# A four-layer preact network on one core: where layer 3 keeps its chain results, and which engine does its small work

## The chip, the cores and the metric

The kernel runs on one core of one Trainium2 chip. The metric is the device time of one execution in microseconds (us), the median of several runs. Five engines work at once, each in the order of its own queue: TensorE (matmuls), VectorE, ScalarE, GpSimd, and SyncE (SP), which here only issues DMA transfers. Matmul results go to PSUM, eight banks of 512 float32 columns per partition; everything else lies in SBUF.

## What is computed

The input x has shape (4, 256, 48, 48), float32. Four layers each add a branch to x, every branch starting with a group norm over 32 groups: layer 0 is cosine attention with 8 heads, layer 1 a gate from pooled depthwise convolutions, layer 2 non-local attention whose output is batch-normalised. Layer 3 is the one that changes:

```python
def _L3_conv_ref(x, attn_w1, attn_w2, refine_w, refine_b):   # x is the group norm's result
    p = jnp.mean(x, axis=(2, 3))
    h = leaky_relu(p @ attn_w1.T, 0.01)
    a = sigmoid(h @ attn_w2.T)                               # a gate for each image and channel
    y = x * a[:, :, None, None]
    y = depthwise_conv3x3(y, refine_w, padding="SAME") + refine_b[None, :, None, None]
    mu = jnp.mean(y, axis=(2, 3), keepdims=True)
    var = jnp.mean(jnp.square(y - mu), axis=(2, 3), keepdims=True)
    y = (y - mu) * rsqrt(var + 1e-5)
    return leaky_relu(y, 0.01)
...
x = x + _L3_conv_ref(_gn(x), ...)
```

## The kernel before, in words

The order of layer 3 is written out by hand: every engine executes its instructions in the order in which the Python code emits them, and semaphores between engines follow the data. An access to a PSUM bank is ordered against every access of another engine to the same bank, whatever the columns.

**Tiles.** Four images times two halves of 128 channels make eight tiles, i = 0 to 7. Two tiles of one image are a pair. A tile is 48 x 48 pixels in six slices of 384 pixels; two slices are a group g, which fills one of three convolution PSUM tiles (`cv_tile`, two banks each). Each bank has 512 columns, of which a slice uses 384.

**A tile's way.** `w_product` (L1504) makes on TensorE what layer 2 adds to a third of a tile, in the PSUM tile `w_all` (rows of the profile call it `w`), of which there is one. `grow` (L1558, VectorE) adds it to x and writes the padded image `pads`; `border` (GpSimd) writes the rim; ScalarE's `square` (L1582) sums squares for the group norm. The padded image is then spread into three shifted copies, `shifted` (`sh`): `spread_out` by eight transfers for each half image from SP (L1596), `keep_here` by copies on VectorE (L1602) or ScalarE (L1598). `products` (L1719) convolves a slice from these copies: 24 small matmuls. ScalarE's `evict` (L1731) and `square` (L1742) take a group out and sum it and its squares; `moments`, `scales`, `shift` (VectorE, with a `pow` on GpSimd at L179) make the scale and offset; `scale` (L1796, ScalarE) applies them; `leak` (L1802) and `gain` (L1807), both VectorE, apply the leaky ReLU and add the block's input; `store` (SP, L1813) writes the group out. The last tile is treated apart: VectorE's `stats` (L1762) reads its moments from PSUM, and nothing is evicted before scaling.

**The chain.** For each pair a `Chain` makes the group norm's scale and the gate in nine short steps: VectorE `total`, TensorE `groups` (L1645), VectorE `inverse`, VectorE `pooled`, TensorE `first_layer` (L1660), VectorE `hidden`, TensorE `second_layer` (L1674), ScalarE `gate`, VectorE `scaled`. The three TensorE results, and that of a check on the attention sums (`judge`, `sound`, L1832 and L1835), lie in `g_tile()`, the last 128 columns of the second bank of `w_all`.

**The schedule.** Time is counted in steps: step t is slice t of the 48 (`CONV`), so tile i begins at step 6 i. `at(t, rank, fn)` puts a piece of work at a step, and within a step the pieces are emitted by rank: FRONT, CONV, PRODUCT, GROW, MID, EVICT, SMALL, MOMENTS, SQUARE, SCALE, LAST, PLACE, STORE. `GATE_AT` gives the steps of the chain against the first step of its pair, `HERE` the steps and engines of the copies, `put_tile` the rest. A tile is prepared by `put_before` 12 steps ahead, a product in each of three steps.

**Before the loop.** Tiles 0 and 1 are prepared in straight code: tile 0's three products into the three convolution tiles, tile 1's first into `w_all` and the others into convolution tiles that have come free. `hum` (L195) issues filler matmuls. The zeros in `shifted` (32 partitions x 2600) are written by GpSimd's memset (L1511, L1856).

**After the loop.** The last tile's statistics and scales come first, then leaks, sums and stores of what is left over from tile 6 (`late`), then those of tile 7.

Of the kernel before, what the change touches and what calls it, by code (L numbers as in the profile page):

```python
# [9 lines left out]
F32 = mybir.dt.float32  # L10
AF = mybir.ActivationFunctionType
# [67 lines left out]
def usual_path(  # L79
# [112 lines left out]
    def hum(out, n):  # L192

        for _ in range(n):
            nc.tensor.matmul(out, lhsT=gmat, rhs=gmat, start=True, stop=True)  # L195
# [1267 lines left out]
    def w_tile():  # L1463
        return [w_all[:, 0, :SL], w_all[:, 1, :SL]]

    def g_tile():
        return w_all[:, 1, SL:]

    def cv_tile():
        return ps_cv.tile([P, 2, 512], F32, tag="cv", name="cv")  # L1470

    def w_pair():
        both = cv_tile()
        return [both[:, 0, :SL], both[:, 1, :SL]]
# [33 lines left out]
        return ps  # L1508


    nc.gpsimd.memset(shifted[0][0:32, 2:4, :], 0.0)  # L1511
    first = [cv_tile() for _ in range(L2C)]
    of_groups = first[L2C - 1][:, 0, SL : SL + B * NK]
    first = [w_product(0, c, [ps[:, 0, :SL], ps[:, 1, :SL]]) for c, ps in enumerate(first)]
    ahead = [w_tile()]
    hum(ahead[0][0][:, :P], 11)

    nc.vector.tensor_mul(sc2, sc2, vec[:, V_G2, :])
    nc.vector.tensor_mul(bi2, bi2, sc2)
# [13 lines left out]
        of_groups, lhsT=gmat, rhs=means.rearrange("p b k -> p (b k)"), start=True, stop=True  # L1533
    )
    w_product(1, 0, ahead[0])
    hum(g_tile(), 5)
    gm = lp.tile([P, B, NK], F32, name="gm")
    edge = lp.tile([P, B, NK], F32, name="edge")
    minus = lp.tile([P, B, NK], F32, name="minus")
    dev = lp.tile([P, B, NK], F32, name="dev")  # L1540
    dev2 = lp.tile([P, B, NK], F32, name="dev2")

    def edges():
        nc.vector.tensor_copy(gm.rearrange("p b k -> p (b k)"), of_groups)
# [7 lines left out]
    def grow(i, c, ps, halves=range(2)):  # L1552

        n, k = TILES[i]
        xs = XT[SEQ[n]][:, k, :].rearrange("p (h r c) -> p h r c", h=2, c=HW)
        to = inside(i, c)
        for h in halves:
            nc.vector.scalar_tensor_tensor(  # L1558
                to[:, h], ps[h].rearrange("p (r c) -> p r c", c=HW),
                sc2[:, k : k + 1], xs[:, h, c * RS : (c + 1) * RS, :], ALU.mult, ALU.add,  # L1560
            )
# [65 lines left out]
    class Chain:  # L1627
# [5 lines left out]
        def steps(self):  # L1633
# [49 lines left out]
            def scaled():  # L1683
# [6 lines left out]
                nc.vector.tensor_mul(self.rsa2, self.rsa, self.rsa)  # L1690

            steps = [
                (MID, total), (SMALL, groups), (FRONT, inverse), (MID, pooled),
                (SMALL, first_layer), (FRONT, hidden), (SMALL, second_layer), (FRONT, gate),
                (FRONT, scaled),
            ]
# [2 lines left out]
    class Conv:  # L1699
# [9 lines left out]
        def products(self, s):  # L1709
            g, h = s // 2, s // L2C  # L1710
            if s % 2 == 0:
                self.ps[g] = cv_tile()
            out = self.ps[g][:, s % 2, :SL].rearrange("p (r c) -> p r c", c=HW)
            sh = shifted[(2 * self.i + h) % 3].rearrange("p j (r c) -> p j r c", c=W2)
            r0 = (s % L2C) * RS
            for dr in range(3):
                for j in range(4):
                    held = slice(0, HELD[j])
                    nc.tensor.matmul(  # L1719
                        out[32 * j : 32 * j + 32], lhsT=made["taps3"][held, self.k, dr, j, :],  # L1720
                        rhs=sh[held, j, r0 + dr : r0 + dr + RS, 0:HW],
                        start=dr == 0, stop=dr == 2,
                    )
# [22 lines left out]

        def moments(self):

            self.mv = mv = small.tile([P, 2], F32, tag="in_mv", name="in_mv")
            nc.vector.tensor_reduce(mv, self.st, AX.X, ALU.add)  # L1750
            nc.vector.tensor_scalar(mv, mv, 1.0 / N, None, ALU.mult)
            d = small.tile([P, 1], F32, tag="in_d", name="in_d")
            nc.vector.tensor_add(d, mv[:, 0:1], self.c)
            ve = small.tile([P, 1], F32, tag="in_ve", name="in_ve")
            nc.vector.scalar_tensor_tensor(ve, d, -1.0, d, ALU.mult, ALU.mult)
            nc.vector.tensor_add(mv[:, 1:2], mv[:, 1:2], ve)

        def stats(self, s):

# [5 lines left out]
            self.mv = small.tile([P, 2], F32, tag="in_mv", name="in_mv")  # L1765
            nc.vector.bn_aggr(self.mv, self.bn.rearrange("p s f -> p (s f)"))

        def scales(self):
            k, ch = self.k, self.chain
            ve = small.tile([P, 1], F32, tag="in_ve2", name="in_ve2")  # L1770
            nc.vector.tensor_scalar(
                ve, self.mv[:, 1:2], ch.rsa2[:, k : k + 1], IN_EPS, ALU.mult, ALU.add
            )
# [4 lines left out]
            rb = vec[:, V_RB, k : k + 1]  # L1778
            nc.vector.scalar_tensor_tensor(
                my, self.mv[:, 0:1], ch.rsa[:, k : k + 1], rb, ALU.mult, ALU.add  # L1780
            )
            self.off = small.tile([P, 1], F32, tag="in_off", name="in_off")
            nc.vector.tensor_sub(self.off, rb, my)

        def shift(self):
            k = self.k
            self.sc = small.tile([P, 1], F32, tag="in_sc", name="in_sc")
            nc.vector.tensor_mul(self.sc, self.chain.rsa[:, k : k + 1], self.ri)
            self.sf = small.tile([P, 1], F32, tag="in_sf", name="in_sf")
            nc.vector.tensor_mul(self.sf, self.off, self.ri)  # L1790

        def scale(self, g, fr=None):
            z = self.cols(g)
# [10 lines left out]
        def gain(self, g):  # L1804
            z = self.cols(g).rearrange("p (r c) -> p r c", c=HW)
            r0 = 1 + 2 * RS * g
            nc.vector.scalar_tensor_tensor(  # L1807
                z, rows_of(self.i)[:, r0 : r0 + 2 * RS, 1 : 1 + HW],
                bi2[:, self.k : self.k + 1], z, ALU.add, ALU.add,
            )  # L1810

        def store(self, g, eng=None):
# [6 lines left out]
    def judge():  # L1819
# [17 lines left out]
        return [(0, MID, lows), (2, SMALL, count), (3, FRONT, compare)]  # L1837

    GATE_AT = {
        0: (3, 4, 5, 5, 8, 9, 10, 11, 12), B - 1: (-2, -1, 0, 0, 2, 3, 4, 5, 6),  # L1840
    }
    for n in range(1, B - 1):
        GATE_AT[n] = (-1, 2, 4, 4, 8, 9, 10, 11, 12)
    chains = [Chain(n) for n in range(B)]
    convs = [Conv(i) for i in range(len(TILES))]

# [5 lines left out]
    grow(0, L2C - 1, first[L2C - 1], [0])  # L1852
    grow(0, 0, first[0], [1])
    spread_first(0)
    for sh in shifted[1:]:
        nc.gpsimd.memset(sh[0:32, 2:4, :], 0.0)  # L1856
    for c in range(1, L2C):
        grow(0, c, first[c], [1])
    spread_first(1)
    centres()  # L1860
    noted[0]()
    for c in range(L2C):
        square(0, c)
    for c in range(L2C):
        grow(1, c, ahead[c])
        if c + 1 < L2C:
            ahead.append(w_product(1, c + 1, w_pair()))
            hum(g_tile(), 3)
        square(1, c)
    border(1)  # L1870


# [11 lines left out]
    def put_before(t, i):  # L1884
# [9 lines left out]
            at(t - 11 + c, SQUARE, lambda c=c: square(i, c))  # L1894
        at(t - 12, PLACE, lambda: border(i))

    late = []
    HERE = [
        (-6, 0, (0, 1), "dve"), (-5, 0, (2, 3), "dve"),
        (-3, 1, (0, 1), "act"), (-3, 1, (2,), "dve"), (-2, 1, (3,), "dve"),  # L1900
    ]

    def put_tile(t, cv, final):
        for s in range(NSL):
            at(t + s, CONV, lambda s=s: cv.products(s))
        if final:
            for s in range(NSL - 1):
                at(t + s + 1, MOMENTS, lambda s=s: cv.stats(s))
            return
        for g in range(NG3):  # L1910
            at(t + 2 * g + 2, EVICT, lambda g=g: cv.evict(g))
            at(t + 2 * g + 3, SQUARE, lambda g=g: cv.square(g))
        at(t + 2, EVICT, cv.centre)
        soon = t + 2 * NSL == T
        t += 0 if soon else 2 if cv.k else 5
# [16 lines left out]
    T = len(convs) * NSL  # L1932
    for i, cv in enumerate(convs):
        t = i * NSL
        put_tile(t, cv, i == len(convs) - 1)
# [875 lines left out]
```

## Time and profile before

| what | us |
|---|---|
| median of 3 runs | 3540.59 (3536.17 to 3544.25) |
| the profiled execution | 3540.24 |
| its span, first to last instruction | 3538.5 |
| layer 3 up to its first convolution slice | 3357.1 to 3380.9 |
| 48 slices | 3380.9 to 3518.3 |
| from the last slice to the end | 3518.3 to 3538.5 |

The profile is one execution. Its page lists busy time by engine, the idle time of an engine ahead of a group of instructions with what released it, and DMA queues; the trace behind it can be asked for a timeline, for waits, for a chain of releases that ended last, and for busy times in given stretches (the windows view). A row such as `PE L1660 MATMUL w<-pm,w 128*64 128x1 f32 x4` is engine, line, operation, output and inputs by the program's names, shape, and count. Names are shared: `x` stands for the images and results, `w` for `w_all` and for weights.

### The profile page before, as it was taken

How to read it: one execution, taken by the hardware profiler on the slowest of the kernel's cores; microseconds unless marked ns; L12 is line 12 of the kernel's file. 1: busy time of each engine (PE TensorE's matmuls, PEld its weight loads, DVE VectorE, ACT ScalarE, POOL GpSimd, SP SyncE). 2: the span in 40 equal slices, each digit the busy share in tenths (PEclk: the TensorE clock that was granted, in tenths of full speed). 3: DMA queues.
4: the chain of work that ended last, by engine and by line, in shares of the span. 5: the costliest groups of instructions: out<-in, count | busy, mean ns of one | idle time of the engine just before them, and what ended most of it. 6: DMA issues, size and time to landing. Idle time of an engine off the chain costs nothing. (4 is left out here: it accounts for less than half of the span.)

```text
span 3538.5 us, 88557 instructions
## 1 busy us (share of the span) xinstructions
PE 3439.1 (97%) x37144; PEld 1743.7 (49%) x37144; DVE 2567.9 (73%) x3523; ACT 2369.3 (67%) x3843; POOL 774.9 (22%) x591
## 2 busy tenths in 40 slices
PE   9999999999999999999999999999999999899986
PEld 5554555454444444444444444444444445565532
DVE  3555545467788788787887886878878868656877
ACT  5665666665886796558867975579668755555465
POOL 2333333321111010010110110110100116666520
PEclk9999999999999999999999999999999999999998
DMA  2211111111111111221111111111111100000066
GB/s 89 49 26 22 26 22 26 22 26 22 27 26 22 26 22 26 56 45 22 26 21 26 21 26 21 26 22 26 22 22 22 22 8 5 5 8 7 4 169 205
DMA packets 121753, 116.62 MB, mean 33 GB/s; under 512 B 58833, under 2 KB 112705, under 8 KB 120577
## 3 DMA queue, kind: packets, MB, share of 16 engines
q1 hardware_dynamic: 120240, 109.16, 16.3%
q8 instruction: 293, 4.80, 0.6%
q10 hardware_dynamic: 1104, 1.71, 0.1%
q14 instruction: 116, 0.94, 0.1%
HBM read 56.99 MB, written 11.80 MB: 19 GB/s over the span
## 5 line engine op out<-in xcount | busy, mean ns | idle before, releaser
L315 ACT ACTIVATE pt<-sc 128x768 f32<-128x768 f32 x1944 | 1475.0, 811 | 731.7 <-PE sc L309 724.1
L355 DVE TENSOR_TENSOR acc<-acc,pt 128x768 f32<-128x768 f32 x1368 | 1370.2, 1002 | 173.7 <-ACT pt L315 74.7
L329 PE MATMUL av<-pt,v 64*64 64x384 f32 x13824 | 1275.7, 484 | 0.0
L309 PE MATMUL sc<-q,k 64*64 64x384 f32 x13824 | 1269.8, 482 | 0.5 <-ACT pt L315 0.5
L309 PEld LDWEIGHTS sc<-q,k 64*64 64x64 f32 x13824 | 524.8, 133 | 590.5 <-issue 544.7
L329 PEld LDWEIGHTS av<-pt,v 64*64 64x64 f32 x13824 | 517.7, 133 | 600.8 <-issue 567.4
L410 POOL TENSOR_TENSOR o<-o,rinv 128x384 f32<-128x384 f32 x95 | 115.6, 1217 | 1729.6 <-DMA rinv<-rinv 1725.2
L340 POOL TENSOR_TENSOR half<-pt 128x768 f32<-128x768 f32 x189 | 365.1, 1935 | 535.8 <-ACT pt L315 496.5
L700 DVE SCALAR_TENSOR_TENSOR x<-pj,bo,x 128x384 f32<-128x384 f32 x192 | 118.5, 617 | 314.4 <-PE pj L687 312.9
L355 DVE TENSOR_TENSOR acc<-acc,half 128x768 f32<-128x768 f32 x171 | 184.1, 1076 | 216.6 <-POOL half L340 216.0
L876 ACT ACTIVATE prod<-pd,wt 128x256 f32<-128x256 f32 x486 | 337.2, 765 | 0.2
L604 PE MATMUL pj<-xs,w 128*128 128x384 f32 (+1 forms) x720 | 275.4, 505 | 0.0
L604 PEld LDWEIGHTS pj<-xs,w 128*128 128x128 f32 x720 | 124.1, 189 | 127.9 <-issue 38.9
L329 PE MATMUL av<-pt,qv 64*64 64x384 f32 x1728 | 176.5, 498 | 0.0
L309 PE MATMUL sc<-qv,kd 64*64 64x384 f32 x1728 | 171.1, 486 | 2.4 <-ACT pt L315 2.4
L899 DVE TENSOR_REDUCE prod<-prod 128x256 f32<-128x1280 f32 x114 | 168.7, 1480 | 0.7 <-ACT prod L876 0.7
L687 PE MATMUL pj<-o,wo 128*128 128x384 f32 (+1 forms) x384 | 160.6, 502 | 5.8 <-issue 3.6
L635 PEld LDWEIGHTS pj<-w,xs 128*128 128x128 f32 x1080 | 134.5, 191 | 24.1 <-issue 1.2
L349 DVE TENSOR_TENSOR acc<-pt 128x768 f32<-128x768 f32 x99 | 112.8, 1140 | 39.8 <-ACT pt L315 39.8
L406 POOL TENSOR_TENSOR o<-raw 128x384 f32<-128x384 f32 x95 | 126.9, 1336 | 52.0 <-ACT raw L402 51.6
L635 PE MATMUL pj<-w,xs 128*128 128x128 f32 x1080 | 134.9, 275 | 0.0
L402 ACT COPY raw<-av 128x768 f32<-128x768 f32 x108 | 86.4, 800 | 48.3 <-PE av L329 44.9
(265 smaller groups left out, 2398.4 us busy)
## 6 DMA issues: line engine op xcount, KB each, us to landing
xs<-in_x_dram SPq DMA_DIRECT2D x90, 384.0 KB
sh<-pad SPq DMA_DIRECT2D x126, 162.2 KB
rinv<-rinv SPq DMA_DIRECT2D x208, 94.5 KB
out_dram<-x SPq DMA_DIRECT2D x24, 384.0 KB
l<-row SPq DMA_DIRECT2D x416, 1.5 KB
w<-in_wqkv_dram SPq DMA_DIRECT2D x32, 192.0 KB
x<-in_x_dram SPq DMA_DIRECT2D x4, 1152.0 KB
x<-in_x_dram SPq DMA_DIRECT2D x9, 384.0 KB
```

The source lines that it names most:

```text
L309: nc.tensor.matmul(ps[c * D : (c + 1) * D, h, :SL], lhsT=u["of"]["k"][r, j0 : j0 + D], rhs=u["of"]["q"][r, u["qc"]], start=True, stop=True,)
L315: nc.scalar.activation(pt, ps[:, :, :SL], AF.Exp, scale=u["scale"])
L329: nc.tensor.matmul(u["av"][h * D : (h + 1) * D, half, :SL], lhsT=value(u, j, h)[r], rhs=pt[r, h, :], start=j == 0, stop=j == JB - 1,)
L340: nc.gpsimd.tensor_add(half, pts[0], pts[1])
L355: nc.vector.tensor_add(u["acc"], u["acc"], term)
L406: eng.tensor_add(u["sum"], u["raw"][:, 0, :], u["raw"][:, 1, :])
L604: nc.tensor.matmul(ps[:, :n], lhsT=at["w"][:, k, t, :], rhs=xs[s][:, k, :n], start=k == 0, stop=k == NK - 1,)
L635: nc.tensor.matmul(ps[:, i * P : (i + 1) * P], lhsT=xs[s][:, k, i * P : (i + 1) * P], rhs=at["w"][:, k, 2, :], start=k == 0, stop=k == NK - 1,
L687: nc.tensor.matmul(ps[:, :n], lhsT=wo[:, p, k * P : (k + 1) * P], rhs=o["o"][:, :n], start=True, stop=True,)
L700: nc.vector.scalar_tensor_tensor(xs, ps[:, :SL], pair["bo"][:, k : k + 1], xs, ALU.add, ALU.add)
L876: nc.scalar.activation(bufs[n % 3][:, :, min(n, 1) + i].rearrange("p (r c) -> p r c", c=AS), pd[:, PAD + dr : PAD + dr + AS, PAD + dc : PA ...
L899: nc.vector.tensor_reduce(to, bufs[n % 3][:, :, : min(n, 1) + len(taps)], AX.X, ALU.add)
```

## The change

All edits are in layer 3.

- `g_tile()` returns the last 128 columns of the second bank of the convolution tile in use instead of those of `w_all`, and the chain's and the check's steps move (`GATE_AT`, `put_chain(13, ...)`), so that their matmuls come after an odd slice. `inverse` has rank MID.
- `moments`, `scales` and `shift` are issued to GpSimd, with each fused operation in two, other than those of the last tile. Steps of scales, leaks and sums move by one to two.
- One of the four copies of a second half image moves from VectorE to ScalarE.
- ScalarE clears the three `shifted` buffers, ahead of everything else, instead of GpSimd.
- Filler falls from 11 to 3 ahead of the means, and the others move; tile 1's products all precede the loop's other work, `centres` comes earlier, and the sums of the last attention rows (`noted`) later.
- Tile 6's leaks, sums and stores all go behind the last slice. Of the six sums there, three (tile 6's groups 1 and 2, tile 7's group 0) leave VectorE: TensorE adds the leaked values and the block's input in PSUM by an identity matrix (`keep_up`, `join`), and ScalarE adds `bi2` and takes them out; the other three stay with `gain`. One store goes out from ScalarE's queue.

```diff
+    cv_last = {}
     def g_tile():
-        return w_all[:, 1, SL:]
+        return cv_last["ps"][:, 1, SL:]
...
-    nc.gpsimd.memset(shifted[0][0:32, 2:4, :], 0.0)
+    for sh in shifted:
+        nc.scalar.activation(
+            sh[0:32, 2:4, :].rearrange("p j c -> p (j c)"),
+            gmat[0:32, 0:1].to_broadcast([32, 2 * CH]), AF.Identity, scale=0.0,
+        )
...
-    hum(ahead[0][0][:, :P], 11)
+    hum(ahead[0][0][:, :P], 3)
...
     w_product(1, 0, ahead[0])
-    hum(g_tile(), 5)
...
+    for c in range(1, L2C):
+        ahead.append(w_pair())
+        hum(ahead[c][0][:, :P], 5 if c == 1 else 1)
+        w_product(1, c, ahead[c])
...
-                (MID, total), (SMALL, groups), (FRONT, inverse), (MID, pooled),
+                (MID, total), (SMALL, groups), (MID, inverse), (MID, pooled),
...
-                self.ps[g] = cv_tile()
+                self.ps[g] = cv_last["ps"] = cv_tile()
...
+            eng, st = nc.gpsimd, self.st
-            nc.vector.tensor_reduce(mv, self.st, AX.X, ALU.add)
-            nc.vector.tensor_scalar(mv, mv, 1.0 / N, None, ALU.mult)
+            eng.tensor_add(mv, st[:, :, 0], st[:, :, 1])
+            eng.tensor_add(mv, mv, st[:, :, 2])
+            eng.tensor_scalar(mv, mv, 1.0 / N, None, ALU.mult)
-            nc.vector.tensor_add(d, mv[:, 0:1], self.c)
-            nc.vector.scalar_tensor_tensor(ve, d, -1.0, d, ALU.mult, ALU.mult)
-            nc.vector.tensor_add(mv[:, 1:2], mv[:, 1:2], ve)
+            eng.tensor_add(d, mv[:, 0:1], self.c)
+            eng.tensor_mul(d2, d, d)
+            eng.tensor_sub(mv[:, 1:2], mv[:, 1:2], d2)
...
-        def scales(self):
+        def scales(self, eng=None):
+            eng = eng or nc.gpsimd
...
+        def onto(self, g, ps, ins, first):
+            for h in range(2):
+                nc.tensor.matmul(
+                    ps[:, h, :SL].rearrange("p (r c) -> p r c", c=HW), lhsT=ident,
+                    rhs=ins[:, h * RS : (h + 1) * RS, :], start=first, stop=not first,
+                )
+        def keep_up(self, g, ps):
+            r0 = 1 + 2 * RS * g
+            self.onto(g, ps, rows_of(self.i)[:, r0 : r0 + 2 * RS, 1 : 1 + HW], True)
+        def join(self, g, ps):
+            self.onto(g, ps, self.cols(g).rearrange("p (r c) -> p r c", c=HW), False)
+            nc.scalar.activation(
+                self.cols(g).rearrange("p (h s) -> p h s", h=2), ps[:, :, :SL], AF.Identity,
+                bias=bi2[:, self.k : self.k + 1],
+            )
...
-        0: (3, 4, 5, 5, 8, 9, 10, 11, 12), B - 1: (-2, -1, 0, 0, 2, 3, 4, 5, 6),
+        0: (3, 5, 6, 7, 9, 10, 11, 12, 13), B - 1: (-2, -1, 0, 0, 3, 4, 5, 6, 7),
-        GATE_AT[n] = (-1, 2, 4, 4, 8, 9, 10, 11, 12)
+        GATE_AT[n] = (-2, 1, 2, 3, 5, 6, 9, 10, 11)
...
-    for sh in shifted[1:]:
-        nc.gpsimd.memset(sh[0:32, 2:4, :], 0.0)
     for c in range(1, L2C):
         grow(0, c, first[c], [1])
+    centres()
     spread_first(1)
-    centres()
-    noted[0]()
...
         grow(1, c, ahead[c])
-        if c + 1 < L2C:
-            ahead.append(w_product(1, c + 1, w_pair()))
-            hum(g_tile(), 3)
         square(1, c)
+    noted[0]()
...
-        (-3, 1, (0, 1), "act"), (-3, 1, (2,), "dve"), (-2, 1, (3,), "dve"),
+        (-3, 1, (0, 1), "act"), (-2, 1, (2,), "act"), (-2, 1, (3,), "dve"),
...
-        t += 0 if soon else 2 if cv.k else 5
+        t += 0 if soon else 1 if i == len(convs) - 3 else 3 if cv.k else 5 if t == 0 else 4
         at(t + 8, FRONT, cv.moments)
-        at(t + 8, FRONT, cv.scales)
+        at(t + 8, MOMENTS, cv.scales)
...
-            if soon and g == NG3 - 1:
-                late.append((cv, g))
+            if soon:
                 continue
-            u = t + 10 + g + (not soon and cv.k)
+            u = t + (10 if t == 5 else 11) + g
...
-    put_chain(14, judge())
+    put_chain(13, judge())
...
-    cv.scales()
-    cv.shift()
+    cv.scales(nc.vector)
+    was = convs[-2]
+    was.leak(0)
+    cv.shift(nc.vector)
     for g in range(NG3):
         cv.scale(g, cv.ps[g])
-    for t in sorted(events):
-        for _, fn in sorted(events[t], key=lambda job: job[0]):
-            fn()
-    for tile, g in late + [(cv, g) for g in range(NG3)]:
-        tile.leak(g)
-        tile.gain(g)
-        tile.store(g)
+    was.keep_up(1, w_all)
+    was.leak(1)
+    was.join(1, w_all)
+    was.leak(2)
+    was.gain(0)
+    was.store(0)
+    was.store(1)
+    cv.leak(0)
+    was.keep_up(2, w_all)
+    cv.keep_up(0, cv.ps[0])
+    was.join(2, w_all)
+    cv.join(0, cv.ps[0])
+    cv.leak(1)
+    cv.gain(1)
+    cv.store(1)
+    was.store(2)
+    cv.leak(2)
+    cv.gain(2)
+    cv.store(2)
+    cv.store(0, nc.scalar)
```

More of the change, by code (lines that the diff above doesn't have):

```diff
@@ L1747, in moments @@
         def moments(self):
+            eng, st = nc.gpsimd, self.st
             self.mv = mv = small.tile([P, 2], F32, tag="in_mv", name="in_mv")
-            nc.vector.tensor_reduce(mv, self.st, AX.X, ALU.add)
-            nc.vector.tensor_scalar(mv, mv, 1.0 / N, None, ALU.mult)
+            eng.tensor_add(mv, st[:, :, 0], st[:, :, 1])
+            eng.tensor_add(mv, mv, st[:, :, 2])
+            eng.tensor_scalar(mv, mv, 1.0 / N, None, ALU.mult)
             d = small.tile([P, 1], F32, tag="in_d", name="in_d")
-            nc.vector.tensor_add(d, mv[:, 0:1], self.c)
-            ve = small.tile([P, 1], F32, tag="in_ve", name="in_ve")
-            nc.vector.scalar_tensor_tensor(ve, d, -1.0, d, ALU.mult, ALU.mult)
-            nc.vector.tensor_add(mv[:, 1:2], mv[:, 1:2], ve)
+            eng.tensor_add(d, mv[:, 0:1], self.c)
+            d2 = small.tile([P, 1], F32, tag="in_d2", name="in_d2")
+            eng.tensor_mul(d2, d, d)
+            eng.tensor_sub(mv[:, 1:2], mv[:, 1:2], d2)
         def stats(self, s):
@@ L1766, in aggregate @@
             nc.vector.bn_aggr(self.mv, self.bn.rearrange("p s f -> p (s f)"))
-        def scales(self):
+        def scales(self, eng=None):
             k, ch = self.k, self.chain
+            eng = eng or nc.gpsimd
             ve = small.tile([P, 1], F32, tag="in_ve2", name="in_ve2")
-            nc.vector.tensor_scalar(
-                ve, self.mv[:, 1:2], ch.rsa2[:, k : k + 1], IN_EPS, ALU.mult, ALU.add
-            )
+            rb = vec[:, V_RB, k : k + 1]
+            if eng is nc.gpsimd:
+                eng.tensor_mul(ve, self.mv[:, 1:2], ch.rsa2[:, k : k + 1])
+                eng.tensor_scalar(ve, ve, IN_EPS, None, ALU.add)
+            else:
+                eng.tensor_scalar(
+                    ve, self.mv[:, 1:2], ch.rsa2[:, k : k + 1], IN_EPS, ALU.mult, ALU.add
+                )
             self.ri = small.tile([P, 1], F32, tag="in_ri", name="in_ri")
@@ L1777, in scales, with shift @@
             my = small.tile([P, 1], F32, tag="in_my", name="in_my")
[L1778 to L1781, printed above, removed]
+            if eng is nc.gpsimd:
+                eng.tensor_mul(my, self.mv[:, 0:1], ch.rsa[:, k : k + 1])
+                eng.tensor_add(my, my, rb)
+            else:
+                eng.scalar_tensor_tensor(
+                    my, self.mv[:, 0:1], ch.rsa[:, k : k + 1], rb, ALU.mult, ALU.add
+                )
             self.off = small.tile([P, 1], F32, tag="in_off", name="in_off")
-            nc.vector.tensor_sub(self.off, rb, my)
-        def shift(self):
+            eng.tensor_sub(self.off, rb, my)
+        def shift(self, eng=None):
             k = self.k
+            eng = eng or nc.gpsimd
             self.sc = small.tile([P, 1], F32, tag="in_sc", name="in_sc")
-            nc.vector.tensor_mul(self.sc, self.chain.rsa[:, k : k + 1], self.ri)
+            eng.tensor_mul(self.sc, self.chain.rsa[:, k : k + 1], self.ri)
             self.sf = small.tile([P, 1], F32, tag="in_sf", name="in_sf")
-            nc.vector.tensor_mul(self.sf, self.off, self.ri)
+            eng.tensor_mul(self.sf, self.off, self.ri)
         def scale(self, g, fr=None):
@@ L1809, in gain @@
                 bi2[:, self.k : self.k + 1], z, ALU.add, ALU.add,
+            )
+        def onto(self, g, ps, ins, first):
[3 more added lines that the diff above has]
+                    rhs=ins[:, h * RS : (h + 1) * RS, :], start=first, stop=not first,
+                )
+        def keep_up(self, g, ps):
[6 more added lines that the diff above has]
+                bias=bi2[:, self.k : self.k + 1],
             )
@@ L1895, in put_before, with put_tile @@
         at(t - 12, PLACE, lambda: border(i))
-    late = []
     HERE = [
         (-6, 0, (0, 1), "dve"), (-5, 0, (2, 3), "dve"),
-        (-3, 1, (0, 1), "act"), (-3, 1, (2,), "dve"), (-2, 1, (3,), "dve"),
+        (-3, 1, (0, 1), "act"), (-2, 1, (2,), "act"), (-2, 1, (3,), "dve"),
     ]
-    def put_tile(t, cv, final):
+    def put_tile(i, t, cv, final):
         for s in range(NSL):
@@ L1934, in usual_path @@
         t = i * NSL
-        put_tile(t, cv, i == len(convs) - 1)
+        put_tile(i, t, cv, i == len(convs) - 1)
         if i > 1:
```

## The prediction

> **What bounds the kernel now.** I read the page first: TensorE is busy 97% of 3538.5 us, but the diff only touches what follows the last attention block, from about 3357 us. So I cut that stretch in the windows view, at the head, the four pairs of tiles (12 steps each, one convolution slice a step) and the tail. Columns: TensorE, weight loads, VectorE, ScalarE, GpSimd busy us (instructions), TensorE clock, DMA share, GB/s.
>
> ```profile
> 3357.10:3380.90 23.80, 14.04 (x112) 8.87 (x112) 18.15 (x44) 9.19 (x14) 16.02 (x14) 0.82 0.42 99
> 3380.90:3413.60 32.70, 31.43 (x351) 12.25 (x354) 18.48 (x36) 21.88 (x41) 1.70 (x5) 0.97 0.67 164
> 3413.60:3454.50 40.90, 33.88 (x356) 12.73 (x352) 32.78 (x70) 28.18 (x49) 4.06 (x7) 0.92 0.75 206
> 3454.50:3493.70 39.20, 32.60 (x352) 14.81 (x344) 32.17 (x66) 28.30 (x50) 2.96 (x5) 0.96 0.85 240
> 3493.70:3518.30 24.60, 24.57 (x297) 9.81 (x296) 22.15 (x58) 16.79 (x28) 2.33 (x4) 1.00 0.64 183
> 3518.30:3538.50 20.20, 0.00 (x0) 0.00 (x0) 14.88 (x23) 4.40 (x5) 0.54 (x1) 0.60 0.38 149
> ```
>
> The same twelve steps take 32.7, 40.9 and 39.2 us; the last pair, which prepares no tile, takes 24.6. TensorE should set the pace and does not. Its timeline says why (the bracket is idle time and releaser):
>
> ```profile
> 3376.24 1.65 PE L195 MATMUL w<-gmat 128*128 128x128 f32 x6 [8.17 <-DVE pad L1558]
> ...
> 3424.84 0.38 PE L1645 MATMUL w<-gn_sq,gmat 128*128 128x2 f32 x2 [2.12 <-DVE pad L1558]
> 3425.16 4.20 PE L1719 MATMUL cv<-sh,taps 96*32 96x384 f32 x48
> ...
> 3444.58 0.59 PE L1660 MATMUL w<-pm,w 128*64 128x1 f32 x4 [3.77 <-DVE pad L1558]
> 3445.10 6.90 PE L1719 MATMUL cv<-sh,taps 96*32 96x384 f32 x48
> ```
>
> Filler (L195) and chain matmuls (L1645, L1660) write a corner of the bank w, and wait until VectorE's `grow` (L1558) has read *other* columns of it. After the 3.77 us wait 48 convolution matmuls take 6.90 instead of 4.08: the wait is paid again in a halved clock.
>
> **What the Trainium skill says.** "PSUM — Partial Sum Buffer", PSUM bank collisions: engines must be kept apart by bank, not by address. The trace agrees: the chain waits for reads of disjoint columns. "TensorE: Matmul & The Clock Gate", What's actually happening: an idle window of some 3.4 us halves the clock. Agrees: 0.50 after 3.77 us, no slowing after 2.12. "SBUF — State Buffer", Who interferes with whom: GpSimd shares a port pair with VectorE's fast copies and two-input operations, and the later one blocks. Agrees: two VectorE copies at 3368.7 us took 1.93 and 2.88 us beside GpSimd instead of 0.83, and GpSimd's border copy 0.92 to 1.00 instead of 0.32. "ScalarE: Activation LUTs", What ACT_TABLE_LOAD costs: an ACTIVATE costs 186 ns + 0.833 ns per element; the 1298-element copy at 1.27 us agrees.
>
> **Head.** ScalarE clears three buffers. By that price 2600 elements are 2.35 us each; three are 7.1 us from 3356.9 (where GpSimd's memset starts now, released by the same VectorE work) to 3364.0. ScalarE is then idle until its copies at 3366.76, so this is free; if it takes 8.5 us it still just fits. Filler of 11 becomes 3 (22 to 6 instructions at 0.12 us: -1.9), which lets the group matmul come when the means are ready; VectorE's 1.09 us wait before L1544 goes. Today the pads are ready for the spread at 3366.7; then 3365.6. All of tile 1's products now precede the loop and no filler waits for L1558: that takes away the 8.17 us wait and the filler and product behind it. What is late next is the spread of the first half: six of its transfers go out from 3365.7; at the 250 GB/s that the DMA moved at 3369 to 3375, 6 x 162 KB is 3.9 us, with about 1 us before the first byte and 1 us after: 3371.6. ScalarE's three copies (3.87 us) end at 3369.5, GpSimd's two (3.24) at 3368.9, TensorE's own queue at 3368.7. Convolution starts at 3371.6 instead of 3380.9: **-9.3 us** (bounds -5 and -10: ScalarE's clears late by 4 us, or an earlier DMA).
>
> **Loop.** Now 3380.9 to 3518.3, 137.4 us. Removed waits of TensorE: first layer 1.27 + 2 x 3.77, groups 2 x 2.12, judge 0.21 + 0.30: 13.6. Removed slow clock: 6.90 - 4.08 = 2.8, and 1.6 after the other 3.77 us wait: 4.4. The initial slow slice (2.96 for 2.14) costs 0.8, which I count as gone since the idle time before it falls from 8 to 3 us. Small product waits (1.3) I leave in. Sum -18.8: 118.6 us, near the bare work: 48 slices x 2.03 + 18 products x 0.81 + chains 4.9 = 116.9. The chain's new places are all after an odd slice, when the convolution bank is complete and its successor is another bank, so its readers hold up nothing but the later eviction.
>
> What then becomes tight, per pair against TensorE's 30.4 us (12 x 2.03 + 6 x 0.81 + 1.2):
> - VectorE: busy 32.5 now. It loses seven or eight small operations per tile, 1.6 to 1.9 us, and one 0.83 us copy: 2 x 2.6 = 5.2, leaving 27.4, plus waits for `pow` of about 1 us.
> - GpSimd gets some 15 tiny operations per tile. No row has such arithmetic; the nearest are border copies at 0.27 to 0.32 and `pow` at 0.55, so 4 to 5 us per tile, up to 15 if every one waits behind a VectorE operation of 1 us. It idles over 85% of the loop. A gain lengthened from 1.02 to 1.11 us beside a border copy gives 0.09 us per GpSimd operation on VectorE: 2 x 17 x 0.09 = 3 per pair (bounds 0 and 0.4 each). VectorE: 31.
> - ScalarE: 28.2 plus two copies of 1.27: 30.8. Evictions have four steps (over 8 us) of room and scales two steps, so its queue may slip 3 to 4 us unseen.
> - DMA: 0.75 x 40.9 + 0.85 x 39.2 = 64 us of service for two pairs, against 61 us. Spreads have six steps, some 14 us, from issue to need, so most is hidden. SP still waits for a store before each reload; queued behind that are eight spreads, with 5 us of room.
>
> All four are near 30 us and coupled through in-order queues. I take 32, 33, 33 and 25 us for the pairs: 123 us, **-14.4** (bounds 117.5 and 133). The moved steps (gates, scales, leaks) are covered by these queues.
>
> **Tail.** At the end of convolution VectorE is now 5.8 us late (last statistics at 3524.12), because tile 6 is leaked and summed among them; its last sum ends at 3533.9, 15.6 us after TensorE. The new order defers tile 6. From the end E of convolution: statistics and aggregate to +1.1, scales +1.7, one leak 0.95, shift at +2.9; ScalarE's three scales 2.8 to +5.8. A join or keep-up on TensorE is two 384-column products of two instructions, 0.33 us each by the start spacing of such rows earlier (L1058: four in 1.4 us), so 1.35 us: join 1 behind leak 1 ends at +5.4, its ScalarE pass (0.81) at +6.8; w is free then, keep-ups to +9.5, join 2 +10.8, join of the last tile +12.2, ScalarE +13.2. VectorE's own leaks and gains end at +10.7. So the last store goes at +13.2 instead of +15.7: **-2.4 us** (-3.5 to +2: at half clock the joins cost 3 to 4 more). Both queues issue single stores; landing and exit, 4.6 us now, stay.
>
> **Sum.** -9.3 - 14.4 - 2.4 = -26.1. The profiled execution took 3540.24 (span 3538.5 and 1.74 around it; the median is 3540.59, so 0.35 apart): 3514.
>
> **Rivals.**
> 1. As above, 3514, own range 3504 to 3522. Chance 0.70.
> 2. ScalarE or DMA becomes the bound: third act copy late, reload late, `grow` waits and so the next product. Pairs of 36 us, and the head at -7: 3514 + 9 + 2 = 3525. For it: DMA share 0.85 already, ScalarE at 101% of TensorE's pace. Against: the room counted above. Chance 0.23.
> 3. Slower: GpSimd's lock. If each of some 34 operations per pair holds VectorE up by its whole `pow`-like time of 0.55 us, a pair is 27.4 + 1 + 18.7 = 47; three pairs give 141, the last 34: 175 us against 137.4, +37.6 - 9.3 - 2.4: 3566. It is slower than now from about 0.37 us per operation. The long VectorE copies in the head speak for it; the 0.09 us in the loop against. Chance 0.04.
> 4. The chain was not what held TensorE: VectorE's 32.5 us and its late `grow` are the true limit and the wait moves to the next product, with head and tail eaten by new order. 3538. Chance 0.03.
>
> **How the numbers follow.** Range 3503 to 3531: from all bounds good (head -10, loop 117.5, tail -3.5: 3507, and 4 us of run scatter as shown by 3536 to 3544) through rival 2 and its spread. About 7 us, 0.2%, is what a measurement can tell from no change: faster 0.93, same 0.03, slower 0.04.
>
> **What would show it.** Right: the first L1719 row near 3371.6; no `w<-pm` or `w<-gn_sq` rows (they name cv), no 2 to 4 us wait on them, clock near 1.0 from the second slice; pairs near 32; last statistics within 1 us of the last matmul. Wrong: waits of products on `grow` over 1 us (VectorE), of `grow` on a reload (DMA), of convolution on ScalarE's copies, GpSimd rows of 1 us beside VectorE rows longer than now; clears that end after 3366 us.

## The result, and the profile after

The changed kernel takes 3526.54 us (median of 6 runs, 3521.92 to 3529.12), the kernel before 3539.21 beside it (6 runs, 3534.63 to 3544.25): ratio 0.9963, 95% interval 0.995 to 0.9975. That is faster by 12.7 us where the prediction had 26. The number lies inside the prediction's range of 3503 to 3531, outside the range of its own case (3504 to 3522) and near what rival 2 would give (3525), but its cause is another.

The profiled execution took 3522.6 us (span 3520.8). The untouched attention part before layer 3 scatters by several us between executions, so I count from the start of the last attention products (TensorE's first row of the form `sc<-y,Ww`: 3357.16 before, 3353.19 after), in three sections:

| us | before | after | difference | predicted |
|---|---|---|---|---|
| to the first convolution slice | 23.73 | 12.82 | -10.9 | -9.3 |
| 48 slices | 137.38 | 130.09 | -7.3 | -14.4 |
| last slice to the end | 20.23 | 24.70 | +4.5 | -2.4 |
| sum | 181.34 | 167.61 | -13.7 | -26.1 |

The first convolution slice begins with two matmuls; in the kernel after, the other 22 wait for a further transfer and start 1.5 us later (in the kernel before all 24 start together). This stretch is counted to the slices.

The windows view of the kernel after, cut as before (head, four pairs, tail; TensorE, weight loads, VectorE, ScalarE, GpSimd busy us with instructions, TensorE clock, DMA share, GB/s):

```profile
3353.20:3366.00 12.80, 9.00 (x84) 4.65 (x85) 10.87 (x33) 10.91 (x7) 5.62 (x6) 1.00 0.26 64
3366.00:3400.30 34.30, 33.59 (x350) 11.95 (x351) 21.68 (x41) 27.53 (x50) 8.09 (x17) 0.95 0.86 201
3400.30:3437.70 37.40, 32.77 (x353) 11.46 (x356) 26.66 (x47) 30.57 (x53) 10.23 (x31) 0.91 0.73 198
3437.70:3469.90 32.20, 30.71 (x354) 10.93 (x344) 27.13 (x44) 27.25 (x47) 17.06 (x33) 1.00 0.99 284
3469.90:3496.10 26.20, 25.58 (x298) 14.39 (x297) 20.00 (x34) 21.99 (x35) 14.53 (x28) 1.00 0.73 225
3496.10:3520.80 24.70, 12.49 (x24) 6.03 (x24) 11.74 (x20) 8.21 (x9) 3.24 (x11) 0.75 0.29 117
```

The pairs take 34.3, 37.4, 32.2 and 26.2 us where I had taken 32, 33, 33 and 25. In the second pair no engine has more than 33 us of work, TensorE's slow clock included, and yet it is 37.4 long: a wait, not an amount of work. VectorE is down to 26.7 from 32.8, GpSimd up by 6 to 14.

The chain's matmuls no longer wait for `grow`. In TensorE's timeline after, in the second pair:

```profile
3406.03 0.38 PE L1656 MATMUL cv<-gn_sq,gmat 128*128 128x2 f32 x2
...
3415.20 0.39 PE L1671 MATMUL cv<-pm,w 128*64 128x1 f32 x4
3415.53 2.14 PE L1730 MATMUL cv<-sh,taps 96*32 96x384 f32 x24
...
3425.18 1.56 PE L1507 MATMUL w<-y,Ww 64*64 64x384 f32 x8 [4.63 <-DVE pad L1569]
3426.66 3.65 PE L1730 MATMUL cv<-sh,taps 96*32 96x384 f32 x24
```

The group sums and the first layer's product, which waited 2.12 and 3.77 us, have no bracket now; one chain matmul, the group sums of the last pair, waits 1.49 us for its own input. But a product (L1507) waits 4.63 us for VectorE's `grow`, and it and the slice behind it run slowly (1.56 instead of 0.88, 3.65 instead of 2.14, at granted clocks of 0.50 and 0.57). The waits view of the loop after says who had held VectorE and ScalarE (total us, times, longest):

```profile
ACT x L1742 <- DVE gn_gv L1660: 11.5, 3, 5.7
...
DVE x L1825 <- ACT x L1819: 8.1, 6, 2.1
```

ScalarE's eviction (L1742) waits for VectorE to have read the group result (`gn_gv`, L1660), which now lies in the convolution bank that the eviction reads; and VectorE's `leak` (L1825) waits for ScalarE's `scale`. The same place in the timelines of ScalarE and VectorE:

```profile
3410.98 0.15 DVE L1660 TENSOR_SCALAR gn_gv<-cv 128x2 f32<-128x2 f32 x1
3411.22 0.81 ACT L1742 ACTIVATE x<-cv 128x768 f32<-128x768 f32 x1 [5.66 <-DVE gn_gv L1660]
3414.23 0.96 DVE L1825 SCALAR_TENSOR_TENSOR x<-x 128x768 f32<-128x768 f32 x1 [2.13 <-ACT x L1819]
...
3423.98 1.14 DVE L1569 SCALAR_TENSOR_TENSOR pad<-w,sc,x 128x384 f32<-128x384 f32 x2 [0.15 <-DMA sh<-pad]
```

Read downwards this is one line of waits: `inverse` (L1660) stands behind copies and a `grow` in VectorE's queue; the eviction waits 5.66 us for it; the scales behind it on ScalarE are late; three leaks on VectorE wait for them (2.13 here, then 0.84 and 1.55); `grow` behind the leaks comes at 3423.98; the next product waits for that. That row itself waits only 0.15 us, for a transfer: it is late because of what stands ahead of it in VectorE's queue.

### The profile page after: what moved, and what is told of

It reads as the page before. It is cut to its first block, busy times and chain, and to the rows that moved or that the text cites. A ratio compares the mean times of both kernels' runs of the same rounds, so it can differ in the third digit from the quotient of the medians.

```text
span 3520.8 us, 88581 instructions
## 1 busy us (share of the span) xinstructions
PE 3439.2 (98%) x37142; PEld 1744.0 (50%) x37142; DVE 2554.3 (73%) x3443; ACT 2387.3 (68%) x3856; POOL 806.6 (23%) x679
```

## The experiments

All are edits of the kernel after, but for the last, which edits the one before. The runs were timed in three batches, in which the kernel before took 3535.83, 3536.79 and 3538.29 us, so ratios compare across them and times don't. Sections are those of the table, each from one profile. The first slice of the loop is 0.8 us slow in most profiles and 2.5 slow in three (after, e1 and e10), with the same head; where I compare slices I take that 1.7 out. The slices of kernels with the same loop then agree within 0.2 us (after and e3; e5 and e10). The timed ratios of most variants lie within each other's intervals, so that the sections decide between them: what follows is a finding about layer 3 in these profiles, not about the timed totals.

**Does the shared bank hold the eviction?** Three runs. The inverse at the front of its step (e1):

```
-   (MID, total), (SMALL, groups), (MID, inverse), (MID, pooled),
+   (MID, total), (SMALL, groups), (FRONT, inverse), (MID, pooled),
```

> Only the rank of the chain's inverse goes back from MID to FRONT, so that VectorE's read of the group result (L1660) comes ahead of the step's grow. Theory W (the new bank wait): ScalarE's evictions, which wait 11.5 us in three pieces for that read, no longer do (under 2 us in all); scales and leaks come earlier, the 4.6 us wait of a product on grow at 3425 us and the slow clock behind it (2.3 us) go. The 48 slices take 122 to 125 us instead of 129.5, and the total falls by 4 to 7 us. Theory S (ScalarE simply has too much work since the third copy): the waits go but the 4.6 us wait stays, since ScalarE's queue is as long; total within 2 us of the changed kernel.

Measured: head 12.85, slices 128.07, tail 23.95, sum 164.87; 3520.12 us, ratio 0.9956 (0.9942 to 0.997). The eviction's waits fall from 11.5 to 6.6 us in all, but in the second pair only from 5.66 to 4.57, since VectorE comes to `inverse` late from its copies as well; the slices gain 2.0, which is neither theory's number. What it does show is in the rows of its timelines, beside those of the run with the moments on VectorE (e6, below):

```profile
3409.92 0.81 ACT L1742 ACTIVATE x<-cv 128x768 f32<-128x768 f32 x1 [4.57 <-DVE gn_gv L1660]
3423.88 1.56 PE L1507 MATMUL w<-y,Ww 64*64 64x384 f32 x8 [3.55 <-DVE pad L1569]
```
```profile
3419.62 0.81 ACT L1742 ACTIVATE x<-cv 128x768 f32<-128x768 f32 x1 [7.50 <-DVE gn_gv L1660]
3434.01 1.56 PE L1507 MATMUL w<-y,Ww 64*64 64x384 f32 x8 [6.57 <-DVE pad L1569]
```

In the second pair eviction wait and product wait go together one for one: 4.57 and 3.55, 5.66 and 4.63 (after), 7.50 and 6.57. The shorter eviction waits of the first and third pair after (2.30 and 3.50 us) have no product wait behind them: there the queues have room. These rows alone would also fit a VectorE that is late for reasons of its own; the next run decides.

The chain's results back in w, its steps staying where the change put them (e5):

```
-        return cv_last["ps"][:, 1, SL:]
+        return w_all[:, 1, SL:]
```

> Only the place of the chain's and the check's results goes back to the last columns of w; their new steps stay. If that place is what held TensorE (as the prediction has it): waits of 1 to 4 us of the chain's matmuls on grow come back in each of the first three pairs (some 8 us and 2 us of slow clock), the evictions' 11.5 us wait goes, and the slices take 132 to 137 us, total 3 to 7 us above the changed kernel. Rival (the moved steps alone remove most of it, since the matmuls of the chain no longer follow products closely, and no eviction waits): slices in 124 to 128 us, total 2 to 5 us below.

Measured: 12.85, slices 126.01, tail 24.36, sum 163.22; 3520.28 us, 0.9957 (0.9943 to 0.9971). No eviction waits for VectorE; TensorE's waits on w are 1.86, 1.39, 1.27 and 0.80 us, against 13.6 before. The first two:

```profile
3408.43 0.38 PE L1656 MATMUL w<-gn_sq,gmat 128*128 128x2 f32 x2 [1.86 <-DVE pad L1569]
...
3423.05 0.88 PE L1507 MATMUL w<-y,Ww 64*64 64x384 f32 x8 [1.39 <-DVE hraw L1678]
```

VectorE's `inverse` even comes later than after (46.2 us behind the start of the first slice instead of 45.0), and yet the `grow` that held TensorE for 4.63 us follows it within 9.7 us instead of 13.0, since the leaks between them wait less for `scale`. So it was the eviction's wait, and not VectorE's own lateness, that made the line of waits and stalled TensorE. The slices are 4.1 us shorter than after's, 2.4 without the first slice's clock. So the new bank is not what took the long waits away; it costs 2.4 us in the loop (2.5 when e10 below is set against e3). The first theory, which was the prediction's, fell here.

The other order, VectorE's reads behind the eviction (e7):

```
-   (SMALL, groups), (MID, inverse), (MID, pooled), (SMALL, first_layer), (FRONT, hidden),
+   (SMALL, groups), (SMALL, inverse), (SMALL, pooled), (SMALL, first_layer), (SMALL, hidden),
-   [(0, MID, lows), (2, SMALL, count), (3, FRONT, compare)]
+   [(0, MID, lows), (2, SMALL, count), (3, SMALL, compare)]
```

> The chain's results stay in the convolution bank at the same steps; only the order within a step changes: inverse, pooled, hidden and the check's compare get rank SMALL, behind the step's eviction, so that VectorE's read waits for ScalarE's eviction and not the other way round. Theory W (what costs the changed kernel its loop time is ScalarE's eviction waiting for VectorE's read in the same bank): the evictions' 11.5 us of waits fall under 2, the 4.6 us wait of a product and the slow clock behind it go, slices in 121 to 125 us instead of 130, layer 3 is 5 to 8 us shorter. Rival S (ScalarE's amount of work, or the reload, decides): waits of L1742 go, but a product still waits 3 us or more for grow, and the slices take over 127 us.

Measured: 12.86, slices 133.24, tail 20.53, sum 166.63; 3525.61 us, 0.9968 (0.9957 to 0.9978). The eviction's 11.5 us are gone, and the wait has turned round. From its timelines, in the last pair:

```profile
3483.16 0.15 DVE L1678 COPY hraw<-cv 64x1 f32<-64x1 f32 x1 [5.27 <-ACT x L1742]
3483.55 1.01 PE L1685 MATMUL cv<-hl,w 64*128 64x1 f32 x4 [5.39 <-DVE hl L1680]
```

Now VectorE waits for the eviction, and TensorE for VectorE. Two engines that only read one bank are still put one behind the other, and whichever is second pays. Against after the slices lose 4.8 us, the first slice's clock taken out, where the theory had them gain. The tail is shorter although the joins are still in it (see the run on the tail, e3, below).

**Is ScalarE's or VectorE's amount of work the limit?** The third copy of a half image back to VectorE (e2):

```
-   (-2, 1, (2,), "act"), (-2, 1, (3,), "dve"),
+   (-3, 1, (2,), "dve"), (-2, 1, (3,), "dve"),
```

> Only the third copy of the second half image goes back from ScalarE to VectorE, at its old step. Theory S: ScalarE has 1.27 us less per tile, 2.5 us per pair, is no longer late, and the 4.6 us wait goes: slices in 122 to 126 us instead of 129.5, total 3 to 6 us less. Theory W: ScalarE still waits some 5 us for VectorE's read in the second pair, the product's wait stays over 3 us, and the total is within 3 us of the changed kernel; VectorE gets 0.83 us per tile more, which can only add.

Measured: 12.95, slices 127.14, tail 23.59, sum 163.68; 3521.4 us, 0.9961 (0.9947 to 0.9975). The eviction waits 5.66 and the product 4.62 us as after; less the first slice's clock the slices gain 1.3. ScalarE's load is not the cause of these waits.

Moments, scales and shift back on VectorE, in their fused form (`tensor_reduce`, `scalar_tensor_tensor`; e6):

```
     # the body of moments goes back as a whole (cut here); in scales and shift:
-   eng = eng or nc.gpsimd
+   eng = eng or nc.vector
```

> Moments, scales and shift go back to VectorE with their fused operations, at the changed kernel's steps; the chain's place and everything else stay. If GpSimd's part is worth what the prediction counted (1.6 to 1.9 us per tile on VectorE, which is near its limit): slices 3 to 6 us longer than in the changed kernel's 130. Rival (VectorE has room, and what counts is that GpSimd's fifteen dependent operations of 0.2 to 1 us make scale and offset late): slices the same or 1 to 4 us shorter, and the tail 2 us shorter, since tile 6's scale no longer waits 5.5 us for GpSimd.

Measured: 12.85, slices 130.48, tail 23.90, sum 167.23; 3528.68 us, 0.9979 (0.9968 to 0.9989). Less the first slice's clock the slices lose 2.0 against after; the tail gains 0.8. The move to GpSimd is worth about 2 us in the loop; the timed ratio puts it at some 6 (0.9979 against 0.9963, intervals that overlap).

**What lengthened the tail?** The last sums back on VectorE, as leak, gain and store for each of the six groups, every store from SP (e3):

```
-    was.keep_up(1, w_all)
-    ...
-    cv.store(0, nc.scalar)
+    for tile, g in [(was, 0), (was, 1), (was, 2), (cv, 0), (cv, 1), (cv, 2)]:
+        if (tile, g) != (was, 0):
+            tile.leak(g)
+        tile.gain(g)
+        tile.store(g)
```

> Only the end: the sums that TensorE and ScalarE do behind the last slice go back to VectorE (leak, sum, store, group by group; tile 6 first), the rest of the new order stays. Theory J (the joins run at half clock and wait for each other): six sums at 1.95 us from the first leak are 11.7 us, the last ends some 17 us after the last slice instead of 19.3, total 2 to 3 us less. Rival (taking three sums off VectorE shortens its queue as meant): the end is 2 to 4 us later than in the changed kernel.

Measured: 12.79, slices 128.59, tail 20.78, sum 162.16; 3519.35 us, 0.9958 (0.9942 to 0.9975). The tail loses 3.9 of its 24.7 us: with this loop VectorE alone is faster than the detour over TensorE. It does not get below the 20.23 us of the kernel before, so putting tile 6 off gained nothing by itself. What the joins cost depends on the wait ahead of them: in e7, whose last slices end later, the first join waits 2.60 us instead of 4.80, one of the six passes runs slowly instead of three, and the tail is 20.53 with the joins in place; taking them out there (e8, below) saves 2.2.

**Combinations.** Reads behind the eviction together with the sums on VectorE (e8), and the same with two copies on ScalarE (e9):

> The new order of e7 and the last sums on VectorE as in e3. If the two causes are separate, the gains add: layer 3 some 9 to 12 us shorter than in the changed kernel (167.6 us from the last attention products to the end), total near 3510 to 3515 when the kernel before takes 3538. If both came from ScalarE's lateness, they overlap: 5 to 8 us.

> As e8, and the third copy of the second half image back on VectorE. If ScalarE's amount of work is the next limit: slices 2 to 4 us shorter than in e8. If VectorE's is: 1 to 4 us longer. If neither (TensorE's own pace is reached): within 1 us.

Measured: heads 12.84 and 12.90, slices 132.76 and 133.16, tails 18.38 and 18.92, sums 163.98 and 164.98; 3523.0 us, 0.9959 (0.9947 to 0.997), and 3521.3, 0.9959 (0.9948 to 0.9971). Layer 3 is 3.6 and 2.6 us shorter than after where 9 to 12 were expected, since e7's part was no gain: the shorter tail holds, the loop stays bad, and ScalarE's third copy makes no difference again.

The edits of e5 and e3 together (chain in w, sums on VectorE; e10):

> Chain results back in the bank w (steps stay moved) and the last sums back on VectorE. Theory: the two losses are independent, one in the loop (shared convolution bank, about 2 to 4 us) and one behind it (joins on TensorE, about 4 us). Then the 48 slices take about 126 us, the stretch behind them about 20.8, layer 3 from the last attention products to the end about 159.6, some 22 us below the kernel before (181.3) and 8 below the changed one (167.6). Rival: both losses come from one cause, a late ScalarE; then undoing both gives no more than the better of the two alone, 162 to 163.

Measured: 12.81, slices 127.82, tail 20.82, sum 161.45; **3517.45 us, 0.9944 (0.9931 to 0.9958)**. With the first slice slow by 2.5 instead of 0.8 the expected 159.6 becomes 161.3: the two losses add, and the rival (one cause) falls. It beats both kernels in the profile (20 and 6 us less in layer 3); timed, it is 20.8 us ahead of the kernel before, and its interval and that of the changed kernel just overlap. Two copies on ScalarE on top of it (e11):

> As the run before, and the third copy of a second half image back from ScalarE to VectorE. Theory: ScalarE's amount of work is not what holds the loop, so within 1 us of the run before (158.6 to 160.6 from the last attention products to the end). Rival: ScalarE's queue is full (a pair has 30.8 us of work for it), so the waits of TensorE on late leaks and sums go, and the slices fall to 122 to 124 us, 156 to 157 in all.

Measured: 12.84, slices 127.88, tail 21.07, sum 161.79; 3519.5 us, 0.9949 (0.9935 to 0.9963). Nothing gained, and without the first slice's clock some 2 us lost, in the third pair (35.9 instead of 33.0).

**What brought the head forward?** On top of e10, the clears back on GpSimd in their old places (e12):

```
-    for sh in shifted:
-        nc.scalar.activation(...)
+    nc.gpsimd.memset(shifted[0][0:32, 2:4, :], 0.0)
...
     spread_first(0)
+    for sh in shifted[1:]:
+        nc.gpsimd.memset(sh[0:32, 2:4, :], 0.0)
```

> Chain in w and last sums on VectorE, and the shifted buffers cleared by GpSimd again, at the places where the kernel before has it. It splits the gain ahead of the loop (10.9 us from the last attention products to the first convolution slice). Theory: it came from the fillers and products that no longer wait behind the padding pass, so the first slice starts 12.8 to 14 us after the last attention products, as without this edit. Rival: it came from the clears: GpSimd is late with its copies and blocks VectorE's, and the first slice starts at 16 to 20 us (before: 23.7).

Measured: head 12.92, slices 127.56, tail 20.47, sum 160.95; 3517.77 us, 0.9944 (0.993 to 0.9957). From its timelines of GpSimd and TensorE (the first clear, the other two, the first slice, and a product in the first pair):

```profile
3358.32 2.37 POOL L1514 MEMSET sh<- 32x2600 f32 x1 [8.46 <-DVE y L410]
3370.24 5.81 POOL L1894 MEMSET sh<- 32x2600 f32 x2
...
3371.47 0.81 PE L1726 MATMUL cv<-sh,taps 96*32 96x384 f32 x2 [1.14 <-DMA sh<-pad]
...
3379.88 0.88 PE L1507 MATMUL w<-y,Ww 64*64 64x384 f32 x8 [1.23 <-DVE pad L1565]
```

The first slice still waits for a spread transfer alone, 12.9 us after the last attention products. The clears brought nothing ahead of the loop. By exclusion the 10.9 us come from the other edits there, in the first place from the fillers and products that no longer wait for `grow` (8.17 us before); less filler and the new places of `centres` and `noted` were not tried alone. In the loop the clears do count: with them on GpSimd, VectorE's two copies (L1609) around the start of the first slice take 3.71 us, in e10 2.63, `grow` behind them is late, a product waits 1.23 us, and the slices, less the first slice's clock, take 1.4 us more than e10's. The timed runs do not tell the two apart.

**The new steps alone.** The kernel before with `GATE_AT`, `inverse`, the rank of `scales` and `put_chain(13, ...)` of the change, and nothing else of it (e13; only the added lines are shown):

```
+    0: (3, 5, 6, 7, 9, 10, 11, 12, 13), B - 1: (-2, -1, 0, 0, 3, 4, 5, 6, 7),
+    GATE_AT[n] = (-2, 1, 2, 3, 5, 6, 9, 10, 11)
+    (MID, total), (SMALL, groups), (MID, inverse), (MID, pooled),
+    at(t + 8, MOMENTS, cv.scales)
+    put_chain(13, judge())
```

> The kernel before with one part of the change alone: the new steps of the chain and of the check, with inverse behind the products and scales behind the chain's pieces; the chain's results stay in w, and everything else as before. Theory: the moved steps made the loop's gain, so the 48 slices take 126 to 129 us instead of 137.4, and the whole kernel gains 8 to 11 us. Rival: the new steps work only with VectorE relieved (moments on GpSimd, a copy on ScalarE); then the slices take 133 to 138.

Measured: head 23.73, slices 136.04, tail 20.88, sum 180.65; 3539.94 us, ratio 1.0004 (0.9995 to 1.0012). No gain: the theory fell; 0.8 of the 1.3 us that the slices are shorter is a first slice at full clock. The second pair of this kernel, and then of e10, in TensorE's timeline:

```profile
3436.69 0.92 PE L1504 MATMUL w<-y,Ww 64*64 64x384 f32 x8 [2.99 <-DVE hraw L1667]
3437.54 3.74 PE L1719 MATMUL cv<-sh,taps 96*32 96x384 f32 x24
```
```profile
3423.79 0.88 PE L1507 MATMUL w<-y,Ww 64*64 64x384 f32 x8 [1.49 <-DVE hraw L1678]
3424.59 2.14 PE L1730 MATMUL cv<-sh,taps 96*32 96x384 f32 x24
```

With the new steps the first layer's matmul (L1660) no longer waits, but the next product waits for VectorE to read its result. In e13 VectorE takes 10.4 us from `gn_gv` to `hraw` (3426.10 to 3436.49), in e10 8.5 (3415.06 to 3423.59). What stands there in addition is ten moment and scale instructions of 0.15 to 0.22 us and a copy of 0.83, while e10 waits 0.71 for a `scale`. So the wait is 2.99 with a slow slice behind it instead of 1.49 with none. The new steps alone bring nothing; together with the other edits they do. That these rows name VectorE's queue speaks for its relief as what was missing, but it was not tried with the new steps alone, nor was the new bank alone. Which of the other edits (moments on GpSimd, later scales and leaks, a copy moved) is worth how much of the 10 us between e13 and e5 is not settled: e6 puts the moments at about 2 in the other bank, e2 and e11 the copy at nothing.

## Why the prediction was right and wrong

**Head (-9.3): right, -10.9, and 0.9 beyond its better bound.** The clears took what they were priced at, and the first slice waits on the spread as foretold; ScalarE and TensorE after:

```profile
3352.84 6.89 ACT L1515 ACTIVATE sh<-gmat 32x2600 f32<-32x2600 f32 x3 [3.34 <-DVE y L410]
3361.55 3.87 ACT L1609 COPY sh<-pad 32x1298 f32<-32x1298 f32 x3 [1.82 <-DVE pad L1569]
...
3367.51 4.44 PE L1730 MATMUL cv<-sh,taps 96*32 96x384 f32 x22 [0.70 <-DMA sh<-pad]
```

6.89 us where 7.1 was foretold, and a ScalarE that then still waits 1.82 for its copies: free, and by e12 without use in the head, though not in the first pair. The prediction let the whole slice wait for the last transfer, 14.4 us after the last attention products. Two matmuls go ahead of it, and the other 22 start at 14.3: by the term that was forecast the gain is 9.4, and the 1.5 us beyond it come back in the first slice. Where the prediction had counted the initial slow slice (0.8 us) as gone, 4.44 us for 22 matmuls is 2.5 us too slow in this execution and 0.8 in most others.

**Loop (-14.4): right that the chain's waits go, half wrong on what remains.** All named waits went, but not by the named cause alone: by e5 they shrink to 5.3 us in the old bank, too. The step that failed is "its readers hold up nothing but the later eviction", with "evictions have four steps (over 8 us) of room". The eviction was seen and priced at nothing. It has room towards TensorE, but in ScalarE's queue scales stand behind it, on which leaks, `grow` and a product depend; the 5.66 us wait came back as 4.63, and about 2.2 of slow clock. The Trainium skill's page "PSUM — Partial Sum Buffer", PSUM bank collisions, which I used for the old bank, holds for the new one just as well; e7 shows it for two engines that both only read. And e5 shows that the place in another bank was not needed once the other edits are there. Of the 7.1 us that the loop lacks against the forecast, the bank's 2.4, the first slice's 1.5 of late matmuls and its 2.5 of slow clock are 6.4; 0.7 is left open.

The prices on GpSimd were too dear for VectorE and a little too cheap for GpSimd. VectorE was to have 31 us a pair, 3 of them lost to GpSimd; it has 26.7 and 27.1. GpSimd was to have 4 to 5 us more a tile; over the loop it has 38.9 more, at least 5.6 for each of seven tiles (part of tile 6's work falls behind it).

**Tail (-2.4): wrong, +4.5.** Two terms failed. From the timelines after, of GpSimd, VectorE, ScalarE and TensorE:

```profile
3494.82 0.92 POOL L1766 TENSOR_TENSOR in_d<-in_mv,in_c 128x1 f32<-128x1 f32 x1
3495.82 0.98 POOL L1768 TENSOR_TENSOR in_d<-in_d 128x1 f32<-128x1 f32 x1
...
3495.73 1.02 DVE L1830 SCALAR_TENSOR_TENSOR x<-pad,bi,x 128x768 f32<-128x768 f32 x1
3496.67 1.95 DVE L1775 BATCH_NORM_STATS2 in_bn<-cv 128x6 f32<-128x384 f32 x4
...
3500.37 0.96 DVE L1825 SCALAR_TENSOR_TENSOR x<-x 128x768 f32<-128x768 f32 x1 [0.69 <-ACT x L1819]
...
3499.31 2.86 ACT L1819 ACTIVATE x<-x,in_sf,in_sc 128x768 f32<-128x768 f32 x3 [5.50 <-POOL in_sf L1813]
3502.39 2.93 PE L1837 MATMUL w<-x,ident 128*128 128x384 f32 x4 [4.80 <-DVE x L1825]
3506.31 2.93 PE L1837 MATMUL w<-pad,ident 128*128 128x384 f32 x4 [0.99 <-ACT x L1849]
3509.03 2.77 PE L1837 MATMUL cv<-pad,ident 128*128 128x384 f32 x4
3511.59 1.50 PE L1837 MATMUL w<-x,ident 128*128 128x384 f32 x4
...
3514.42 0.90 ACT L1849 ACTIVATE x<-cv,bi 128x768 f32<-128x768 f32 x1 [0.39 <-PE cv L1837]
```

First, the statistics. They were to end 1.1 us after convolution (at 3496.1) and end 2.5 after it, because leaks and sums of tile 5 now stand ahead of the last four in VectorE's queue: putting tile 6 off did not clear that queue. And "one leak 0.95" took tile 6's values as scaled by then. Their moments run on GpSimd from 3493.95, behind ScalarE's last square, to 3499.27, and ScalarE waits 5.50 us for them; VectorE, which is late itself, loses only 0.69 us to that. Together they delay the first join, which begins 6.3 us after convolution instead of 4.05. That GpSimd does the work is the smaller part: with the moments on VectorE (e6) the first join still waits 4.63 us instead of 4.80.

Second, "1.35 us" for a join or keep-up is a price at full clock (1.45 to 1.56 measured); after that wait three of five cost 2.93, 2.93 and 2.77, 4.6 us more together, with a granted clock of 0.50, as the bracket in the prediction had held possible ("at half clock the joins cost 3 to 4 more"). The last sum ends at 3515.32, 19.2 us after convolution instead of 13.2 (the two terms make 6.9; the steps overlap more closely than I had them, by 0.9), and the end follows 5.5 us later, not 4.6. e3 shows the joins' share: without them 3.9 us less.

**Rivals.** Rival 2 (3525) met the number, and its late `grow` ahead of a late product did come, but not from its cause: a copy off ScalarE left the waits (e2, e11), and the pair with DMA at 0.99 is the shortest of those that prepare tiles. That the total came so near it is chance, made of a better head, a longer loop and a longer tail. Rival 3 did not come: no lengthening of VectorE near 0.37 us for each GpSimd instruction. Rival 4 was closer than its 0.03: in e13 the wait moves to the next product and the time stays (3539.94), as it said; with the other edits it is wrong.

## What to carry to other kernels

When a result moves to another PSUM bank to escape a wait, list every engine that touches the new bank and what stands behind each of them in its queue: two readers of a bank wait for each other, and a "later eviction" is priced at nothing only when nothing behind it feeds TensorE. Work that is put on an idle TensorE at the end of a kernel is to be priced at half clock as well: here one to three of six passes ran so. Edits of one schedule need not add up: the moved steps brought nothing alone, so a gain should be tried in parts before it is put down to one of them.

## What was unexpected of the hardware

- GpSimd's tiny arithmetic (128 x 1 or 2 elements) takes 0.19 us alone and 0.92 to 1.04 beside VectorE's two-input operations on 768 columns; VectorE's own stay at 0.94 to 1.02. The Trainium skill's page "SBUF — State Buffer", Who interferes with whom, says that the order of issue decides who blocks. That agrees with the two rows shown above: they start 0.06 and 0.09 us behind a leak and a sum of VectorE's and end 0.04 and 0.05 behind them. So the price fell to GpSimd, while I had put 3 us a pair on VectorE. In the head VectorE does pay: its two copies take 2.63 us beside GpSimd's copies (e10) and 3.71 beside its clears (e12), instead of 1.65.
- The halved clock doesn't follow from the length of the last wait alone: after 1.87 us a slice took 3.16 us (e10, granted clock 0.65), after 2.72 us it took 2.14 (e13, clock 1.00), and after the same head it was slow by 0.8 or 2.5. The Trainium skill's page "TensorE: Matmul & The Clock Gate", What's actually happening, has the window free-running, so that the same kernel starts with a different number of slow matmuls; the 0.8 and 2.5 agree.
- Where layer 3 begins differs by several us between executions of unchanged code (3352.37 to 3361.37 in these profiles): differences of that size are not to be read from absolute times of one profile.
